# A convolution layer on one core: the order in which bursts of matmuls are written down in layer 1

## The chip, the cores and the metric

The kernel runs on 1 core of one Trainium2 chip. The metric is the device time of one execution, in microseconds (us); the time before is the median of three runs. One more execution was recorded by the hardware profiler: its instructions with their times are the trace, and a page made from it is the profile. The engines are named as there: PE is TensorE (PEld its weight loads), DVE VectorE, ACT ScalarE, POOL GpSimd, SP SyncE, which here only issues DMAs.

## The reference, cut to what matters

Two layers work on `x` of 16 images, 16 channels, 256 x 256 pixels. Layer 0 is a spectral layer (Fourier transforms and residues) and isn't touched. Layer 1 is this, with `B, C, H, W = 16, 16, 256, 256` and `H2 = 128`:

```python
xs = x.reshape(B * C, 1, H, W)                       # x: the group norm of layer 0's output
f = mish(conv2d(xs, W1, b1))                         # 1 -> 4 features, 3x3
top, bot = (f[:, :, :H2], f[:, :, H2:])
ker = conv2d(jax.nn.relu(conv2d(bot, Wred, bred)), Wspan, bspan)     # 4 -> 1 -> 9, 1x1
patches = jax.lax.conv_general_dilated_patches(top, (3, 3), (1, 1), [(1, 1), (1, 1)], ...)
patches = patches.reshape(B * C, 4, K2, H2, W)
top_inv = (patches * ker[:, None]).sum(axis=2)       # the involution
...
shuffled = jnp.concatenate([ti, jnp.roll(bo, -1, axis=1)], axis=3)
shuffled = shuffled.reshape(B, 4 * C, H, W)
out = mish(conv2d(shuffled, W2, b2))                 # 64 -> 16 channels, 3x3
pooled = out.mean(axis=(2, 3))
gate = jax.nn.sigmoid(...)                           # three taps of pooled over the channels
return x * gate[:, :, None, None]
```

The output is `x` plus this. All of it is in 32-bit floats.

## The kernel before

Layer 1 works image by image (`b`), each in nine units (`s` = 0 to 8). One pass of the loop at L1404 is called a step here. A step does one unit of three things at once: the first convolution of the next unit (`nxt`), the involution of this unit (`now`), and one eighth of the second convolution of the image before (`conv2(b - 1, s, acc)`, not in step 8). The first image's steps have no second convolution, the last image's second convolution runs alone at the end in another form (`conv2_last`). Step 8 also begins the gate of the image before (`gated`), whose remaining parts run over the next steps, and makes the first planes of this image (`fresh`).

What TensorE does in a step comes in bursts, each with one shape of array tile:

- `convolve(turn)`, L1130, twice: 24 matmuls with 18 rows and 64 columns of the array, into four PSUM banks (`c1`, in the trace `c`). ScalarE applies mish to the four banks: two into `bot` (L1153), two into `wide` (L1161).
- `involution(kernel)`, L1185, twice: 48 matmuls of 32 x 32 into four banks (`pd`). VectorE multiplies them by `r` into `t` (kernel 0, L1209) or adds `t` to them into `top` (kernel 1, L1211). Kernel 1 then issues `store_top`, eight DMAs on POOL's queue.
- four products, L1268, in `conv2`: 8 matmuls each of 128 x 32 into one bank (`c2ps`). The three taps of a row are computed for pairs of pixels from four planes: differences and sums of neighbouring columns, made by `plane` on VectorE (L1263, two instructions each), with four sets of weights. Product 1 is copied by ScalarE into `a` (L1296), `even` and `odd` gather the four products on VectorE (L1303, L1304, L1307, L1311), and `pooled` (L1286) applies mish to them on ScalarE and sums them up. `following(k)` makes plane `k` for the next step, and may overwrite it once product `k` has read it.
- `reduce`, L1165: 8 matmuls of 64 x 32 into two banks (`pr`), the sum over the rows of `bot`. ScalarE makes `r` of them (L1182), and `store_bot` issues its DMAs on POOL's queue.

A matmul of 32-bit floats is two instructions in the trace, so a product has 16 there, a turn 48, an involution kernel 96.

All these outputs come from one pool of eight PSUM banks, tag `bank` (L1040), in rotation: the ninth request waits until the first bank has been read out. A step with products asks for 4 x 4 + 4 + 2 = 22.

Inside `tc.manual_schedule` (L1397) the order on PE, ACT, DVE and POOL is the order in which the Python code writes instructions down; each engine works its own queue in that order, and semaphores join them where data do. In the kernel before, `conv2` is a generator: at each `yield` it hands back to the loop, which writes something else in between. In this way each product stands between two bursts of other work. `pooled(odd, 1)` is written in the next step, by `next(first, None)`. SP's queue holds `load_rows` (`z`, eight DMAs a unit, three buffers, issued two units ahead by `begin_unit`), `conv2_rows` (one DMA for the rows of a later step, two buffers, so it waits for the planes that read the old ones) and the gate's loads `o`.

Of the kernel before, what the change touches and what calls it, by code (L numbers as in the profile page):

```python
# [10 lines left out]
F32 = mybir.dt.float32  # L11
# [10 lines left out]
P = 128  # L22
# [1001 lines left out]
def layer1(ctx, tc, d, zn, cf, mr, nb):  # L1024
# [8 lines left out]
    H = N // 2  # L1033
# [3 lines left out]
    rp = ctx.enter_context(tc.tile_pool(name="l1r", bufs=3))  # L1037
    op = ctx.enter_context(tc.tile_pool(name="l1o", bufs=4))
    sm = ctx.enter_context(tc.tile_pool(name="l1s", bufs=2))
    banks = ctx.enter_context(tc.tile_pool(name="banks", bufs=8, space=PSUM))  # L1040

    def bank(shape, name):
        return banks.tile([P, *shape], F32, tag="bank", name=name)
# [203 lines left out]
    def conv2_rows(b, s):  # L1247
        t = rows2[(8 * b + s) % 2]
        flat = cf[b % 4].rearrange("(t y) f c x -> (y f c) t x", y=2)
        nc.sync.dma_start(out=t[:, :, 1 : N + 1], in_=flat[:, 16 * s : 16 * s + 17])  # L1250

    def plane(b, s, k):

        t = rows2[(8 * b + s) % 2]
        before, odd, even, after = (t[:, :, x : x + H] for x in (0, 1, H + 1, H + 2))
        x, y, op_ = (
            (before, odd, ALU.subtract),
            (odd, even, ALU.add),
            (odd, even, ALU.subtract),
            (even, after, ALU.subtract),  # L1260
        )[k]
        for rows in (slice(0, 9), slice(9, 17)):
            nc.vector.tensor_tensor(planes[:, k, rows], x[:, rows], y[:, rows], op_)  # L1263

    def conv2(b, s, acc):

        def products(terms):
            ps = bank([4, H], "c2ps")  # L1268
            for i, (w, src) in enumerate(terms):
                for blk in range(2):  # L1270
                    for j in range(4):
                        nc.tensor.matmul(  # L1272
                            ps[32 * j : 32 * j + 32],
                            lhsT=w[:, blk],
                            rhs=src[:, 4 * j + blk : 4 * j + blk + 4],
                            start=(i, blk) == (0, 0),
                            stop=(i, blk) == (len(terms) - 1, 1),
                        )
            return ps

        def product(k):
            return products([(weights[k], planes[:, k])])

        def pooled(y, q):
            k = 2 * s + q
            nc.scalar.activation(y, y, AF.Mish, bias=b2, accum_out=acc[:, k : k + 1])  # L1286

        def following(k):
            if s < 7:
                plane(b, s + 1, k)  # L1290

        if b == nb - 1:
            yield from conv2_last(b, s, products, pooled)
            return
        a = rp.tile([P, 4, H], F32, tag="mid", name="mid", bufs=2)
        nc.scalar.copy(a, product(1))  # L1296
        following(1)
        yield
        ps = product(2)
        even = rp.tile([P, 4, H], F32, tag="even", name="even", bufs=2)  # L1300
        odd = rp.tile([P, 4, H], F32, tag="odd", name="odd", bufs=2)
        yield
        nc.vector.tensor_tensor(even, ps, a, ALU.add)  # L1303
        nc.vector.tensor_tensor(odd, a, ps, ALU.subtract)  # L1304
        following(2)
        yield
        nc.vector.tensor_tensor(even, product(0), even, ALU.add)  # L1307
        following(0)
        yield
        pooled(even, 0)  # L1310
        nc.vector.tensor_tensor(odd, odd, product(3), ALU.subtract)  # L1311
        following(3)
        yield
        pooled(odd, 1)
        yield

    def conv2_last(b, s, products, pooled):

        t = rows2[(8 * b + s) % 2]
        nc.vector.tensor_tensor(pair, t[:, :, H + 1 :], t[:, :, : H + 1], ALU.add)  # L1320
        nc.scalar.copy(mid[:, :, :H], products([(c2[:, :, 1], t[:, :, H + 1 : N + 1])]))
        ps = products([(c2[:, :, 0], t[:, :, :H]), (c2[:, :, 2], t[:, :, 1 : H + 1])])
        even = rp.tile([P, 4, H], F32, tag="even", name="even", bufs=2)
        nc.vector.tensor_tensor(even, ps, mid[:, :, :H], ALU.add)
        odd = rp.tile([P, 4, H], F32, tag="odd", name="odd", bufs=2)
        nc.vector.tensor_tensor(odd, ps, mid[:, :, 1:], ALU.add)
        pooled(even, 0)
        ps = products([(c2[:, :, 0], pair[:, :, :H]), (w12, pair[:, :, 1:])])
        nc.vector.tensor_tensor(odd, ps, odd, ALU.subtract)
        pooled(odd, 1)  # L1330
        yield

    def gate(b, acc):

# [55 lines left out]
    def begin_unit(i):  # L1390
        if i < len(order):
            b, n = order[i]
            units[i] = Unit(b, i, n)

    E = mybir.EngineType
    with tc.manual_schedule(engines={E.PE, E.Activation, E.DVE, E.Pool}):
        begin_unit(0)  # L1397
        begin_unit(1)
        u = units[0]
        u.convolve(0)  # L1400
        u.convolve(1)
        u.reduce()
        acc, last, first, second = None, iter(()), iter(()), iter(())
        for i in range(9 * nb + 12):  # L1404
            b, s = divmod(i, 9)
            now, nxt = units.pop(i, None), units.get(i + 1)
            begin_unit(i + 2)
            if s >= 7 and b < nb:
                conv2_rows(b, s - 7)
            if b == nb and 0 < s < 7:  # L1410
                conv2_rows(b - 1, s + 1)
            if s < 6 and 0 < b < nb:
                conv2_rows(b - 1, s + 2)
            fresh = s == 8 and b < nb - 1
            gated = s == 8 and 0 < b <= nb
            next(last, None)
            if nxt:
                nxt.convolve(0)
            if s < 8 and b and b <= nb:
                if s == 0:  # L1420
                    acc = sm.tile([P, 16], F32, tag="acc", name="acc")
                second = conv2(b - 1, s, acc)
            if now:
                now.involution(0)
            next(first, None)
            next(second, None)
            if now:
                now.involution(1)
            if fresh:
                plane(b, 0, 1)  # L1430
            next(second, None)
            if gated:
                last = gate(b - 1, acc)
                next(last)
            if nxt:
                nxt.convolve(1)
            next(second, None)
            if fresh:
                plane(b, 0, 2)
            next(second, None)  # L1440
            if fresh:
                plane(b, 0, 0)
            if nxt:
                nxt.reduce()
            next(second, None)
            if gated:
                next(last)
            if fresh:
                plane(b, 0, 3)
            if gated:  # L1450
                next(last)
            next(last, None)
            first, second = second, iter(())

# [143 lines left out]
@with_exitstack  # L1600
def forward(ctx, tc, d):
    nb = d["x"].shape[0]
    dram = ctx.enter_context(tc.tile_pool(name="dram", bufs=1, space=DRAM))
    keep = ctx.enter_context(tc.tile_pool(name="keep", bufs=1))
    al = dram.tile([17, 4, 2, C, nb, 2, N], F32, name="al")
    bd = dram.tile([nb, P, P], F32, name="bd")
    hd = dram.tile([2, 2, 64, 2, nb // 2, C, N], F32, name="hd")
    tabs = (
        dram.tile([P, C // 2, 4, N], F32, name="td"),
        dram.tile([NF, P, 384], F32, name="avd"),  # L1610
        dram.tile([P, 2, C, N], F32, name="ed"),
    )
    zn = dram.tile([nb, N + 2, C, N + 2], F32, name="zn")
    cf = dram.tile([4, N + 2, 4, C, N], F32, name="cf")
    mr = keep.tile([P, nb, G, 2], F32, name="mr")
    layer0_forward(tc, d, al, bd, tabs)
    layer0_mix(tc, d, al, hd, tabs)
    layer0_back(tc, d, hd, bd, zn, mr, tabs[2])
    layer1(tc, d, zn, cf, mr, nb)
# [25 lines left out]
```

## Time and profile before

| what | us |
|---|---|
| time before, median of 3 runs (5986.34 to 6002.63) | 5996.09 |
| profiled execution, its own time | 6010.53 |
| its span, first to last instruction | 6008.8 |
| layer 1 in it, 2930.0 to 6008.8 | 3078.8 |
| of which PE busy / DVE busy | 2984.7 / 2282.5 |
| of which ACT busy / POOL busy | 1137.6 / 1512.4 |
| 14 images in their steady course, 3264.7 to 5878.6 | 2613.9 |
| the last image's end, 5878.6 to 6008.8 | 130.2 |

The 16 DMA engines are busy 83% of layer 1 on average, and the mean granted clock of TensorE over the span is 0.978 of full speed. Busy shares are means over stages with different limits; one line of the timeline is a run of equal instructions, with its start, its length and, in brackets, the time that its engine stood idle before it and what ended that. The length of a run of matmuls includes the modelled end of the last one, so the next run can begin before it is over; durations of bursts are therefore taken from start to start.

### The profile page before, as it was taken

What the parts mean: (1) busy time and instruction counts of PE and PEld (TensorE: products, weight loads), DVE (VectorE), ACT (ScalarE), POOL (GpSimd) and SP (SyncE); (2) the same over time, 40 slices, a digit from 0 to 9 for tenths busy, and PEclk for the clock granted to TensorE, in tenths of its full rate; (3) what the DMA queues carried; (4) which work ended last, traced back from release to release, by engine and by line L of the source; (5) the groups of instructions that cost most, each with busy time, mean ns of one, the idle gap of its engine ahead of it and who ended that gap; (6) DMA issues with size and microseconds to landing.
All of it is one profiled execution on the core that took longest, in us unless ns stands there. A gap on an engine that the chain in (4) does not pass through costs nothing.

```text
span 6008.8 us, 216283 instructions
## 1 busy us (share of the span) xinstructions
PE 5572.9 (93%) x94280; PEld 3166.7 (53%) x94280; DVE 4666.5 (78%) x8643; ACT 2310.8 (38%) x4158; POOL 2802.4 (47%) x4090
## 2 busy tenths in 40 slices
PE   6999999688988888999899999999999999999996
PEld 5888888576766766777433333333333333333332
DVE  8888888388887876888557787777877778777784
ACT  2344556344444442222233333333333333333331
POOL 1344444333333335666544555544555445544453
PEclk9999999899999999999899999999999999999998
DMA  3455555566565658999677888888888888888886
GB/s 96 142 141 160 164 143 144 159 189 199 193 200 190 194 193 294 326 327 326 216 217 217 280 269 268 251 242 272 271 267 251 243 268 279 264 250 251 262 278 225
DMA packets 814469, 1370.07 MB, mean 228 GB/s; under 512 B 139824, under 2 KB 629168, under 8 KB 798384
## 3 DMA queue, kind: packets, MB, share of 16 engines
q1 hardware_dynamic: 596176, 881.61, 46.5%
q0 software_dynamic: 217344, 474.61, 25.8%
q8 instruction: 741, 12.14, 0.8%
q14 instruction: 208, 1.70, 0.1%
HBM read 729.78 MB, written 556.47 MB: 214 GB/s over the span
## 4 chain that ended last, share of the span: by engine, by line
PE 66%; DVE 20%; DMA 8%; issue 4%; ACT 1%; POOL 1%; SPq 1%; DVEq 0%; ACTq 0%; POOLq 0%
PE pd L1194 16%; PE c2ps L1272 15%; PE c L1144 12%; DMA z<-in_x 5%; PE ph L760 4%; PE ps L706 3%; PE pg L725 3%; PE pr L1172 2%; DVE planes L1263 2%; PE py L951 2%; PE py L952 2%; DVE st L167 2%; PE pt L741 2%; DVE zb L983 1%; DVE st L968 1%
## 5 line engine op out<-in xcount | busy, mean ns | idle before, releaser
L1224 POOL DMA_DIRECT2D cf<-top x1152 | 668.3, 692 | 1162.8 <-DVE top L1211 987.0
L1263 DVE TENSOR_TENSOR planes<-rows 128x1152 f32<-128x1152 f32 x960 | 1203.4, 1295 | 0.1
L1194 PE MATMUL pd<-wide,dw 32*32 32x512 f32 x27648 | 1032.8, 599 | 32.8 <-issue 17.6
L1153 ACT ACTIVATE bot<-c,b 128x512 f32<-128x512 f32 x576 | 364.8, 684 | 1450.9 <-PE c L1144 1099.4
L1144 PE MATMUL c<-z,w 18*64 18x512 f32 x13824 | 835.1, 601 | 15.7 <-DMA z<-zn 15.7
L1194 PEld LDWEIGHTS pd<-wide,dw 32*32 32x32 f32 x27648 | 446.6, 103 | 595.7 <-issue 455.5
L1209 DVE TENSOR_TENSOR t<-pd,r 128x512 f32<-128x512 f32 x576 | 357.5, 682 | 482.3 <-PE pd L1194 481.7
L1144 PEld LDWEIGHTS c<-z,w 18*64 18x64 f32 x13824 | 293.2, 132 | 533.4 <-issue 410.8
L1242 POOL DMA_DIRECT2D cf<-bot x720 | 395.4, 622 | 198.3 <-DMA cf<-top 81.2
L780 POOL TENSOR_TENSOR h<-w 128x256 f32<-128x256 f32 x258 | 211.4, 820 | 583.7 <-DVE w L774 580.8
L1272 PE MATMUL c2ps<-planes,c 128*32 128x512 f32 x3968 | 477.1, 598 | 0.0
L1211 DVE TENSOR_TENSOR top<-pd,t 128x512 f32<-128x512 f32 x576 | 357.4, 682 | 106.4 <-PE pd L1194 106.1
L1369 POOL TENSOR_SCALAR o<-o,scale,mean 128x258 f32<-128x258 f32 x488 | 355.5, 736 | 155.9 <-DVE scale L1361 141.5
L964 POOL TENSOR_TENSOR x<-x,o 128x512 f32<-128x512 f32 x256 | 324.5, 1268 | 215.1 <-DVE o L963 215.1
L205 PE MATMUL pu<-fy,f 128*128 128x128 f32 x2048 | 414.8, 285 | 1.1 <-ACT u L219 1.0
L212 PE MATMUL pv<-at,f 128*128 128x128 f32 x2048 | 403.1, 279 | 0.0
L322 POOL DMA_DIRECT2D al<-o x544 | 338.3, 629 | 118.1 <-ACT o L313 79.2
L1161 ACT ACTIVATE wide<-c,b 128x512 f32<-128x512 f32 x576 | 365.0, 693 | 0.0
L725 PE MATMUL pg<-alb,s 128*32 128x64 f32 x16896 | 288.0, 222 | 70.7 <-issue 52.3
L706 PE MATMUL ps<-tt,lt 64*32 64x256 f32 x8448 | 292.3, 388 | 54.0 <-issue 20.5
L951 PE MATMUL py<-h,iy 128*128 128x256 f32 x1024 | 316.4, 391 | 10.7 <-DMA h<-hd 10.7
L760 PE MATMUL ph<-ix,yt 64*128 64x128 f32 x4128 | 294.2, 281 | 31.2 <-DVE w L774 22.0
(244 smaller groups left out, 9937.8 us busy)
## 6 DMA issues: line engine op xcount, KB each, us to landing
rows<-cf SPq DMA_DIRECT2D x128, 2176.0 KB
cf<-top POOLq DMA_DIRECT2D x896, 112.0 KB, 5.5
cf<-bot POOLq DMA_DIRECT2D x336, 224.0 KB, 6.4
z<-zn SPq DMA_DIRECT2D x576, 129.0 KB
alb<-alx SPq DMA_DIRECT2D x132, 512.0 KB
zn<-zb SPq DMA_DIRECT2D x128, 516.0 KB
o<-zn SPq DMA_DIRECT2D x128, 516.0 KB
z<-in_x SPq DMA_DIRECT2D x64, 1024.0 KB
```

The source lines that it names most:

```text
L205: nc.tensor.matmul(pu[:, h, :, :, e].rearrange("p v g m -> p (v g) m"), lhsT=f[:, e, c, h], rhs=fy[:, e].rearrange("p (n m) -> p n m", m=2 ...
L212: nc.tensor.matmul(pv[:, a, h], lhsT=f[:, e, c, h], rhs=at[:, e, 4 * cg + c].rearrange("p l m -> p (l m)"), start=e == 0, stop=e == 1,)
L706: nc.tensor.matmul(ps[32 * g : 32 * g + 32, odd, v], lhsT=lt[lanes, kk, g, 1 - v : 3 - v].rearrange("p l c -> p (l c)"), rhs=tt[lanes, kk, g],
L725: nc.tensor.matmul(ps[32 * q : 32 * q + 32, x], lhsT=s[:, i].rearrange("p v k -> p (v k)"), rhs=alb[:, :, column(i)], start=True, stop=True,)
L760: nc.tensor.matmul(ph[q][:, e, blocks], lhsT=yt[lanes, i].rearrange("p t k -> p (t k)"), rhs=ix[lanes, i].rearrange("p (b x) -> p b x", b= ...
L951: nc.tensor.matmul(py[:, e], lhsT=iy[:, e], rhs=h[:, e, k % 4], start=True, stop=False)
L1144: nc.tensor.matmul(ps[half, a][to : to + 64], lhsT=w1[lanes, dx], rhs=self.z[lanes, c : c + 2, dx : dx + N], start=dx == 0, stop=dx == 2,)
L1194: nc.tensor.matmul(out[32 * k : 32 * k + 32], lhsT=dw[lanes, kernel, dx], rhs=self.feat[lanes, 2 * k : 2 * k + 2, dx : dx + N], start=dx == 0,
L1224: nc.gpsimd.dma_start(out=rows[y + 2 * lo : y + 2 * hi, :, c + 2 * k : c + 2 * k + 2].rearrange("y f c x -> y f (c x)"), in_=o[32 * k + 2 ...
L1242: nc.gpsimd.dma_start(out=rows[y + 4 * lo : y + 4 * hi, to : to + n].rearrange("p c x -> p (c x)"), in_=src.rearrange("p c q x -> p (c q x)"),
L1263: nc.vector.tensor_tensor(planes[:, k, rows], x[:, rows], y[:, rows], op_)
L1272: nc.tensor.matmul(ps[32 * j : 32 * j + 32], lhsT=w[:, blk], rhs=src[:, 4 * j + blk : 4 * j + blk + 4], start=(i, blk) == (0, 0), stop=(i, ...
```

## The change

`conv2` loses its `yield`s and is a plain function that writes its four products one after the other, with the sums of `even` and `odd` and both `pooled` between them; the planes 2, 0 and 3 for the next step are written after both. The loop writes the convolution's two turns, then the involution's two kernels, then (in step 8) the gate's second part and the four planes of this image, then `conv2`, then `reduce`. The gate's first part moves to the head of step 8, ahead of the turns, and its matmul `pg` ahead of `reduce`. `pooled(odd, 1)` is no longer put off to the next step. No instruction is added or taken away.

```diff
-            yield from conv2_last(b, s, products, pooled)
+            conv2_last(b, s, products, pooled)
             return
         a = rp.tile([P, 4, H], F32, tag="mid", name="mid", bufs=2)
+        even = rp.tile([P, 4, H], F32, tag="even", name="even", bufs=2)
+        odd = rp.tile([P, 4, H], F32, tag="odd", name="odd", bufs=2)
         nc.scalar.copy(a, product(1))
         following(1)
-        yield
         ps = product(2)
-        even = rp.tile([P, 4, H], F32, tag="even", name="even", bufs=2)
-        odd = rp.tile([P, 4, H], F32, tag="odd", name="odd", bufs=2)
-        yield
         nc.vector.tensor_tensor(even, ps, a, ALU.add)
         nc.vector.tensor_tensor(odd, a, ps, ALU.subtract)
-        following(2)
-        yield
         nc.vector.tensor_tensor(even, product(0), even, ALU.add)
-        following(0)
-        yield
         pooled(even, 0)
         nc.vector.tensor_tensor(odd, odd, product(3), ALU.subtract)
-        following(3)
-        yield
         pooled(odd, 1)
-        yield
+        for k in (2, 0, 3):
+            following(k)
...
-        acc, last, first, second = None, iter(()), iter(()), iter(())
+        acc, last = None, iter(())
...
-            fresh = s == 8 and b < nb - 1
             gated = s == 8 and 0 < b <= nb
             next(last, None)
-            if nxt:
-                nxt.convolve(0)
-            if s < 8 and b and b <= nb:
-                if s == 0:
-                    acc = sm.tile([P, 16], F32, tag="acc", name="acc")
-                second = conv2(b - 1, s, acc)
-            if now:
-                now.involution(0)
-            next(first, None)
-            next(second, None)
-            if now:
-                now.involution(1)
-            if fresh:
-                plane(b, 0, 1)
-            next(second, None)
             if gated:
                 last = gate(b - 1, acc)
                 next(last)
             if nxt:
+                nxt.convolve(0)
                 nxt.convolve(1)
-            next(second, None)
-            if fresh:
-                plane(b, 0, 2)
-            next(second, None)
-            if fresh:
-                plane(b, 0, 0)
+            if now:
+                now.involution(0)
+                now.involution(1)
+            if gated:
+                next(last)
+            if s == 8 and b < nb - 1:
+                for k in (1, 2, 0, 3):
+                    plane(b, 0, k)
+            if s < 8 and b and b <= nb:
+                if s == 0:
+                    acc = sm.tile([P, 16], F32, tag="acc", name="acc")
+                conv2(b - 1, s, acc)
             if nxt:
                 nxt.reduce()
-            next(second, None)
-            if gated:
-                next(last)
-            if fresh:
-                plane(b, 0, 3)
             if gated:
                 next(last)
             next(last, None)
-            first, second = second, iter(())
```

More of the change, by code (lines that the diff above doesn't have):

```diff
@@ L1330, in conv2_last @@
         pooled(odd, 1)
-        yield
     def gate(b, acc):
```

## The prediction

> **What bounds it now.** I read the page first: engine shares, then the chain that ended last.
>
> ```profile
> PE 5572.9 (93%) x94280; PEld 3166.7 (53%) x94280; DVE 4666.5 (78%) x8643; ACT 2310.8 (38%) x4158; POOL 2802.4 (47%) x4090
> PE 66%; DVE 20%; DMA 8%; issue 4%; ACT 1%; POOL 1%; SPq 1%; DVEq 0%; ACTq 0%; POOLq 0%
> ```
>
> TensorE carries the chain, but both lines cover two layers, and only layer 1 (2930 to 6009 us) is edited. So I read the timeline of TensorE over one ordinary step (columns: start, length, engine, line, operation, count).
>
> ```profile
> 4512.06 2.83 PE L1144 MATMUL c<-z,w 18*64 18x512 f32 x48
> 4514.82 3.40 PE L1194 MATMUL pd<-wide,dw 32*32 32x512 f32 x96
> 4518.16 1.92 PE L1272 MATMUL c2ps<-planes,w_sum 128*32 128x512 f32 x16
> 4520.01 3.40 PE L1194 MATMUL pd<-wide,dw 32*32 32x512 f32 x96
> 4523.35 1.92 PE L1272 MATMUL c2ps<-planes,w_difference 128*32 128x512 f32 x16
> 4525.20 2.83 PE L1144 MATMUL c<-z,w 18*64 18x512 f32 x48
> 4527.96 1.92 PE L1272 MATMUL c2ps<-planes,c 128*32 128x512 f32 x16
> 4529.81 1.09 PE L1172 MATMUL pr<-bot,wr 64*32 64x512 f32 x16
> 4530.83 1.92 PE L1272 MATMUL c2ps<-planes,c 128*32 128x512 f32 x16
> 4532.69 0.69 PE L1144 MATMUL c<-z,w 18*64 18x512 f32 x8
> ```
>
> No line has an idle time: each burst starts as the last one ends, and the step is 4532.69 - 4512.06 = 20.63 us. From start to start, a convolution turn (C) takes 2.76, an involution kernel (I) 3.33, a product (P) 1.85, the sum over rows (R) 1.02. Over the same 20.6 us VectorE is busy 17.05 and ScalarE 8.1. So only shorter TensorE work can shorten such a step, and the number of matmuls doesn't change. What is left is the seam between bursts.
>
> **Price of a seam.** Where the old kernel already has equal bursts together, a seam can be read: two involution kernels in a step without products, three products in the last image.
>
> ```profile
> 3267.47 6.60 PE L1194 MATMUL pd<-wide,dw 32*32 32x512 f32 x192
> 3274.00 2.83 PE L1144 MATMUL c<-z,w 18*64 18x512 f32 x48
> ...
> 5898.87 5.43 PE L1272 MATMUL c2ps<-rows,c 128*32 128x512 f32 x48
> 5904.07 1.95 PE L1272 MATMUL c2ps<-planes,c 128*32 128x512 f32 x16
> 5905.78 1.95 PE L1272 MATMUL c2ps<-planes,w 128*32 128x512 f32 x16
> ```
>
> Two I together: 6.53, against 2 x 3.335 = 6.67, so 0.14 for the seam. Products together: 5905.78 - 5904.07 = 1.71 against 1.855, so 0.145. For C-C no warm row exists; within a turn the weight loads follow each other by 0.43, six of these are 2.58 of the 2.76, so its seam is between 0 and 0.18. I take 0.145, what the other two have. The new step is C C, I I, P P P P, R: nine bursts become four, five seams go: 5 x 0.145 = 0.725, and the step becomes 19.90.
>
> **Do the new neighbours wait?** All matmul outputs share 8 PSUM banks in rotation. I put C at 0, then C 2.61, I 5.37, I 8.6, P from 11.9, R 18.9. The ends come from rows of the old step: ScalarE starts on a turn 2.84 after its start (4525.20, 4528.04):
>
> ```profile
> 4528.04 1.27 ACT L1153 ACTIVATE bot<-c,b 128x512 f32<-128x512 f32 x2 [7.28 <-PE c L1144]
> 4529.19 1.27 ACT L1161 ACTIVATE wide<-c,b 128x512 f32<-128x512 f32 x2
> ```
>
> - The first I takes the banks of the first C. Fourth bank free at 2.84 + 1.15 + 1.27 = 5.26, plus 0.06 (old waits resume TensorE that soon): 5.32, needed 5.37. It fits by 0.05. Bounds: 0 to 0.15 lost per step; I take 0.
> - The second I takes the second C's: 5.46 + 2.42 = 7.9, needed 8.6.
> - VectorE: t 8.83 to 11.3 (3.46 after the first I starts, as at 4514.82/4518.28), top 11.9 to 14.4, plane 1 to 16.9, the four sums to 19.8, planes 2, 0, 3 to 27.2, which is 7.3 of the next step; t is due there at 8.8. Slack 1.5. Planes 2, 0, 3 are read from 13.6 on, so they are early.
> - Second C of the next step takes the banks of P0, P3 and R. R's are read last, behind both pooled activations: odd sum 19.8, pooled to 20.7, r to 21.9; needed 22.5.
>
> The Trainium skill (Trainium Kernel Development and Optimization, Best Practices) speaks against the change: tiling speeds TensorE up, not the emptying of PSUM, and two turns together fill all eight banks. By that rule the involution would wait for the whole eviction; by the rows above ScalarE empties the first four while the second turn runs. The rule's sum is my slow rival; the rows' is 0.05 to spare.
>
> **Queues passed.** SP's rows load waits for plane 3 of the step before, so it moves from 2.7 to 7.3 in its step, but its reader (plane 1, one step on) moves from 8.6 to 14.4: the lead stays about 26 us. z loads behind it lead by over a step. POOL keeps its order; store_top comes at 13.6, store_bot after R. The gate's sum moves to the head of the step, which saves 0.2 of TensorE's wait per image.
>
> **Turn of the image** (steps 8, 0, 1). Old: 15.0 (3264.71 to 3279.71), 23.94 (to 3303.65), then 20.6. New step 8: 5.37 + 6.53 + 0.3 (pg) + 1.02 = 13.2, since R no longer stands behind the second turn's activation (2.4 there, 1.02 behind other work). But VectorE is late: top ends 14.4, the gate's 16 small operations to 17.7, eight plane halves (9.9) to 27.6, scale to 28.3, that is 15.1 into step 0. t is due at 8.8 and starts at 15.1; the first product takes t's bank, so it waits from 12.0 to 15.8. That is an added wait of 3.9 us; behind it on TensorE stand all products, R and the next turn. Step 0: 15.8 + 6.98 + 1.02 = 23.8. By that alone step 1 would lose 1.2, because R's banks come late to its second C.
>
> A gap that long also costs clock, as an instruction gap in the first image shows (windows: start:end, length, busy and count of five engines, clock, DMA share, GB/s):
>
> ```profile
> 3025.95 1.47 PE L1194 MATMUL pd<-wide,dw 32*32 32x512 f32 x33 [2.22 <-issue]
> 3027.34 5.08 PE L1144 MATMUL c<-z,w 18*64 18x512 f32 x48
> ...
> 3028.90:3032.40 3.50, 3.50 (x42) 0.82 (x28) 0.81 (x2) 0.01 (x1) 3.50 (x7) 0.50 0.79 198
> ```
>
> After 2.22 us idle the granted clock is 0.50 for some 6 us: C takes 5.08 for 2.83, R 2.82 for 2.44, 2.6 lost. A gap of 1.29 at 3058.8 cost as much, one of 0.91 at 2979.5 nothing. The skill's rule (TensorE: Matmul & The Clock Gate, HAM oscillation) is that gaps above about 3.4 us halve the clock for a window of 3.4, which would cost 1.7. The row decides: 2.6. Step 0 becomes 26.4; then R comes so late that step 1's wait for R's banks is covered, and step 1 is 19.9. Turn: -1.8 + 2.5 - 0.7 = 0. Without the clock drop it would be -1.8 - 0.1 + 0.5 = -1.4.
>
> **First image, 8 steps without products.** Old 14.43 (2989.34 to 3003.77). New 5.37 + 6.53 + 1.02 + 0.25 (the first C waits for the second I's bank) = 13.15. Saved 1.28 each. **Last image**: bursts unchanged, rows wait for DMA there; 0 (at most 3, where pg waited for the sum).
>
> **Sum.** Steps 2 to 7 of 15 images: 90 x 0.725 = 65. Turns: 15 x 0 = 0. First image: 8 x 1.28 = 10. Together 75 of the profiled span: 6008.8 to 5934, execution 6010.5 to 5935.5. The median shown is 14 below that execution; the same 75 off 5996 gives **5921**, 1.25% less.
>
> **Rivals.**
> - *DMA caps the steps behind the gate.* For: after a turn the DMA engines are full:
>
> ```profile
> 3303.65:3324.50 20.85, 20.64 (x372) 7.10 (x368) 16.93 (x21) 7.62 (x16) 14.01 (x23) 1.00 1.02 333
> ```
>
>   Against: outside the last image no plane ever waited for rows. If three steps an image can't shorten: 15 x 3 x 0.725 = 33 back, 5954. Chance 0.12.
> - *The turn eats the gain.* The gap in step 0 longer, or VectorE's lag still there in steps 2 and 3: 5 us per image give all of it back, 5996. Against: VectorE regains 2.3 us per step. 0.08.
> - *ScalarE doesn't free the first turn's banks before the second turn ends* (slower). Then the fourth bank comes at 5.46 + 2.42 = 7.9, I waits 2.5, in every one of 143 steps: 358 lost less 75, 6279, and more if the clock falls. It decides from 0.7 us of lateness per step. Against: the old ScalarE starts within 0.1 of a turn's end with the next burst already running. 0.12.
> - *Seams cost the same whatever stands beside* contradicts the rows above; it lies in the second rival's result.
>
> **Chances.** Forecast 0.68, the rivals 0.12, 0.08, 0.12. Forecast's bounds: no clock drop 21 lower, C-C seam at 0.18 another 4; 0.15 at the first I, 20 higher. With the DMA case on top of that: 5892 to 5976. Faster by over 0.3% (about what can be told from no change): 0.68 + 0.12 = 0.80; same 0.08; slower 0.12.
>
> **What would show it.** In an ordinary step: period 19.9, 96 c, 192 pd, 64 c2ps matmuls in unbroken runs, no idle at the first pd. In step 0: c2ps idle about 3.9 behind t, clock 0.5 after it. In the first image 13.2. Wrong if pd waits for ACT wide by more than 0.7, or planes wait for rows.

## The result

| | us |
|---|---|
| kernel before, median of 4 runs (5973.89 to 6002.63) | 5991.22 |
| changed kernel, median of 4 runs (5903.02 to 5926.36) | 5913.39 |
| ratio, 95% interval | 0.9874 (0.9841 to 0.9906) |
| profiled execution of the changed kernel, and its span | 5909.9, 5908.1 |

The forecast was 75 us less; the medians differ by 78. The page of the changed kernel, the same two lines as before:

```profile
PE 5447.1 (92%) x94280; PEld 3319.2 (56%) x94280; DVE 4671.7 (79%) x8643; ACT 2324.0 (39%) x4158; POOL 2831.1 (48%) x4090
PE 55%; DVE 10%; issue 2%; DMA 1%; ACT 1%; POOL 0%; SPq 0%; DVEq 0%; ACTq 0%; POOLq 0%
```

The instruction counts are the same, to the last one. TensorE is busy 126 us less, which is not faster matmuls: the tail of a run's last matmul covers the seam behind it, so a seam counts as busy time, and there are fewer seams. The span is 100.7 us shorter, so TensorE is also idle for 25 us more. An ordinary step in the changed kernel's timeline of TensorE:

```profile
3102.90 5.41 PE L1144 MATMUL c<-z,w 18*64 18x512 f32 x96
3108.24 6.60 PE L1194 MATMUL pd<-wide,dw 32*32 32x512 f32 x192
3114.77 1.92 PE L1272 MATMUL c2ps<-planes,w_sum 128*32 128x512 f32 x16
3116.51 1.90 PE L1272 MATMUL c2ps<-planes,w_difference 128*32 128x512 f32 x16
3118.22 3.62 PE L1272 MATMUL c2ps<-planes,c 128*32 128x512 f32 x32
3121.77 1.09 PE L1172 MATMUL pr<-bot,wr 64*32 64x512 f32 x16
3122.79 5.41 PE L1144 MATMUL c<-z,w 18*64 18x512 f32 x96
```

3122.79 - 3102.90 = 19.89 us, and no line has an idle time. Start to start: two turns 5.34 (2 x 2.76 = 5.52 before), two involution kernels 6.53 (6.67), four products 7.00 (7.42), the sum 1.02. The five seams are worth 0.18 + 0.14 + 0.42 = 0.74.

A usual turn of an image, from the head of step 8 to the head of step 1:

```profile
5232.97 5.41 PE L1144 MATMUL c<-z,w 18*64 18x512 f32 x96
5238.31 6.60 PE L1194 MATMUL pd<-wide,dw 32*32 32x512 f32 x192
5244.84 0.39 PE L1345 MATMUL pg<-wca,totals 128*128 128x16 f32 x2
5245.16 1.09 PE L1172 MATMUL pr<-bot,wr 64*32 64x512 f32 x16
5246.18 6.00 PE L1144 MATMUL c<-z,w 18*64 18x512 f32 x96
5252.11 6.60 PE L1194 MATMUL pd<-wide,dw 32*32 32x512 f32 x192
5261.63 3.62 PE L1272 MATMUL c2ps<-planes,w_sum 128*32 128x512 f32 x16 [2.92 <-DVE t L1209]
5265.03 1.94 PE L1272 MATMUL c2ps<-planes,w_difference 128*32 128x512 f32 x16
...
5271.35 5.41 PE L1144 MATMUL c<-z,w 18*64 18x512 f32 x96
```

Step 8 takes 13.21. In step 0, 25.17 long, the first product waits 2.92 us for VectorE's `t`, and then takes 3.40 instead of 1.7. The clock behind that wait, in the windows view (the third last number):

```profile
5261.58:5265.18 3.60, 3.55 (x20) 0.99 (x24) 3.60 (x7) 0.00 (x0) 3.26 (x7) 0.53 0.98 332
```

Where the 100.7 us between the two spans came from:

| stretch | before | after | difference |
|---|---|---|---|
| up to layer 1's first step (the code is the same) | 2955.7 | 2940.7 | -15.0 |
| first image, steps 0 to 7 | 127.6 | 108.9 | -18.8 |
| its step 8, and the second image to its step 8 | 181.4 | 172.7 | -8.8 |
| 14 images from step 8 to step 8 | 2613.9 | 2559.5 | -54.4 |
| end of the last image | 130.2 | 126.4 | -3.8 |

The first row isn't the change's: it varies from one execution to the next, and a later kernel with the old order (E2) had 2934.6 there. That leaves 86 us in layer 1. The first image gained 18.8, and not the 10 forecast, because the old execution had three steps there of 16.3, 19.7 and 19.3 us with instruction gaps like the one that the prediction showed; of the new steps one has such a gap (16.1), the others take 12.9 to 13.6.

By step, the mean over 13 images (head of one step to the next; the last of the 14 isn't complete):

| step | 8 | 0 | 1 | 2 | 3 | 4 | 5 | 6 | 7 | sum |
|---|---|---|---|---|---|---|---|---|---|---|
| before | 15.07 | 23.99 | 21.30 | 20.92 | 21.47 | 21.27 | 21.23 | 20.71 | 20.84 | 186.80 |
| after | 13.47 | 24.71 | 21.40 | 21.13 | 20.95 | 20.63 | 20.32 | 19.91 | 20.15 | 182.67 |

Seams alone would give 0.74 in each of the steps 1 to 7. Steps 6 and 7 have it; steps 1 to 4 have little of it.

### The profile page after: what moved, and what is told of

Its sections match the earlier page's. It is cut to its first block, busy times and chain, and to the rows that moved or that the text cites. A ratio compares the mean times of both kernels' runs of the same rounds, so it can differ in the third digit from the quotient of the medians.

```text
span 5908.1 us, 216564 instructions
## 1 busy us (share of the span) xinstructions
PE 5447.1 (92%) x94280; PEld 3319.2 (56%) x94280; DVE 4671.7 (79%) x8643; ACT 2324.0 (39%) x4158; POOL 2831.1 (48%) x4090
## 4 chain that ended last, share of the span: by engine, by line
PE 55%; DVE 10%; issue 2%; DMA 1%; ACT 1%; POOL 0%; SPq 0%; DVEq 0%; ACTq 0%; POOLq 0%
PE c2ps L1272 15%; PE pd L1194 15%; PE c L1144 12%; DVE planes L1263 2%; PE pr L1172 2%; PE py L951 2%; PE py L952 2%; PE ph L760 2%; PE ps L706 2%; DVE zb L983 1%; DVE st L968 1%; PE pg L725 1%; PE pf L940 1%; PE pt L741 1%; DVE o L963 1%
## 5 line engine op out<-in xcount | busy, mean ns | idle before, releaser
L1263 DVE TENSOR_TENSOR planes<-rows 128x1152 f32<-128x1152 f32 x960 | 1180.4, 1293 | 7.0 <-PE c2ps L1272 6.9
L1194 PE MATMUL pd<-wide,dw 32*32 32x512 f32 x27648 | 988.6, 597 | 28.2 <-issue 28.0
L1144 PE MATMUL c<-z,w 18*64 18x512 f32 x13824 | 801.5, 595 | 16.2 <-DMA z<-zn 15.8
L1194 PEld LDWEIGHTS pd<-wide,dw 32*32 32x32 f32 x27648 | 542.2, 103 | 459.4 <-issue 175.2
L1144 PEld LDWEIGHTS c<-z,w 18*64 18x64 f32 x13824 | 319.6, 131 | 491.0 <-issue 352.0
L1361 POOL TENSOR_SCALAR o<-o,scale,mean 128x258 f32<-128x258 f32 x488 | 386.1, 799 | 151.6 <-DVE scale L1353 133.6
L1272 PE MATMUL c2ps<-planes,c 128*32 128x512 f32 x3968 | 454.7, 594 | 3.4 <-DVE planes L1313 3.4
L1298 ACT COPY mid<-c2ps 128x512 f32<-128x512 f32 x120 | 70.5, 588 | 867.3 <-PE c2ps L1272 867.3
```

Source lines behind the costliest of these rows:

```text
L1144: nc.tensor.matmul(ps[half, a][to : to + 64], lhsT=w1[lanes, dx], rhs=self.z[lanes, c : c + 2, dx : dx + N], start=dx == 0, stop=dx == 2,)
L1194: nc.tensor.matmul(out[32 * k : 32 * k + 32], lhsT=dw[lanes, kernel, dx], rhs=self.feat[lanes, 2 * k : 2 * k + 2, dx : dx + N], start=dx == 0,
L1272: nc.tensor.matmul(ps[32 * j : 32 * j + 32], lhsT=w[:, blk], rhs=src[:, 4 * j + blk : 4 * j + blk + 4], start=(i, blk) == (0, 0), stop=(i, ...
L1361: eng.tensor_scalar(o[:, i], o[:, i], scale[:, c + i : c + i + 1], mean2[:, b, c + i : c + i + 1], ALU.mult, ALU.add,)
```

## The experiments

The theory is the prediction's: the gain is the seams, five in an ordinary step; the turn is held up by VectorE's lag and the clock. The rivals: the gain comes from waits that went, not from seams; the turn is bound by something else; the steps behind the gate are bound by the DMA engines. In each run the period of an ordinary step is that of the undisturbed steps, the commonest length, which repeats to 0.01 us.

**E4, E8: seams put back one by one.** In `conv2` of the changed kernel:

```diff
         following(1)
+        yield                      # E4: C C I P I P P P R
         ps = product(2)
...
+        between()                  # E8: nxt.reduce(), C C I I P P R P P
         nc.vector.tensor_tensor(even, product(0), even, ALU.add)
```

> The changed kernel with product 1 put back between the two involution kernels: C C I P I P P P R, six bursts for four. Seams: one of I-I and one of P-P more, 0.14 each: an ordinary step takes 20.17 for 19.89. Rival (the step shortened because waits went, not because of the seams): no wait comes back here, so 19.89.

> The changed kernel with the sum over rows put between products 2 and 0: C C I I P P R P P, five bursts for four. One seam more: an ordinary step takes 20.03 for 19.89. Rival (waits, not seams): 19.89, since R's input and its banks are ready there.

Measured: 20.17 and 20.03, both to the hundredth. With the changed kernel's 19.89 at four bursts and the old 20.63 at nine, the step follows the number of bursts, 0.14 to 0.15 for each. Neither run brought a wait back in these steps. Times of one execution each: 5946.9 and 5915.0.

**E5, E6: is it the shape?** Ahead of products 2, 0 and 3 one more small matmul, once of the products' shape, once of another:

```diff
+            if k != 1:
+                extra = bank([4, H], "extra")
+                nc.tensor.matmul(extra[:32, 0], lhsT=weights[0][:, 0], rhs=planes[:, k, 0], start=True, stop=True)
```

E6 has `[:32, 0]` and `[:32, k, 0]` for the two operands.

> The changed kernel with one added matmul of 128 columns ahead of products 2, 0 and 3, of the products' own tile shape (128 rows, 32 columns of the array), into a bank that nobody reads. This is the control of the next run: the added matmuls cost their own length, at most 3 x 0.21 us, so an ordinary step takes 20.0 to 20.6.

> As the control, but the three added matmuls use 32 rows of the array instead of 128. If the seam is the price of another tile shape, each of them opens one or two seams of 0.14 that the control doesn't have: an ordinary step is 0.4 to 0.85 us longer than the control's. If the seam belongs to the boundary between two operations whatever their shapes, the two runs agree within 0.05.

Measured: 20.53 with the same shape (0.213 for each added matmul, its own length), 21.30 with the other: 0.77 more, or 0.26 for each pair of seams (one execution each, 5962.0 and 6050.2). So it is the change of shape, and not the boundary between two operations. The weight loads show how. In the timeline of TensorE's weight loads (here of E1) the first load of a burst of another shape comes 0.84 after the last, one of the same shape 0.30:

```profile
3795.43 0.16 PEld L1272 LDWEIGHTS c2ps<-planes,w_sum 128*32 128x32 f32 x8 [0.84 <-DVE t L1209]
...
3796.75 0.13 PEld L1272 LDWEIGHTS c2ps<-planes,w_difference 128*32 128x32 f32 x4 [0.30 <-DVE top L1211]
```

The first line is the seam from involution to product, the second the boundary between product 1 and 2; both first loads have a releaser named, and only one costs. The 0.30 is also the distance within one product. The loads of product 2 thus begin 0.43 ahead of its first matmul in the ordinary step above (3116.08 and 3116.51); those of product 1, behind the seam, begin with it (3114.76 and 3114.77).

**E7: how much room has ScalarE?** One more copy between the two pairs of mish of the first turn:

```diff
+            if turn == 0:
+                spare = rp.tile([P, 4, H], F32, tag="spare", name="spare", bufs=1)
+                nc.scalar.copy(spare, self.bot[:, 0:2].rearrange("p c e x -> p (c e) x"))
             for a in range(2):
```

> The changed kernel with one more copy on ScalarE (about 0.59 us) between the two pairs of mish of the first turn. Theory: the involution needs the first turn's fourth bank only 0.05 us after it is free, so an ordinary step becomes 0.5 us longer, 20.4. Rival (the banks have room): 19.89.

Its ordinary step in the timeline of TensorE:

```profile
4525.84 5.41 PE L1144 MATMUL c<-z,w 18*64 18x512 f32 x96
4531.17 7.05 PE L1197 MATMUL pd<-wide,dw 32*32 32x512 f32 x192
```

The involution starts as soon, but its run is 0.45 longer, since its fourth bank comes late: 20.34 (20.4 forecast, 19.89 by the rival). In all undisturbed steps of the changed kernel that bank is free 5.31 us into the step, and the first matmul into it runs at 5.36; with the copy it is free at 5.78, and the matmul runs at 5.79. The room was 0.05, as forecast. One execution took 5945.8.

**E1, E3: VectorE's lag in the turn.** The planes of the next image are made in step 7, all four (E1) or plane 1 alone (E3):

```diff
-            if s == 8 and b < nb - 1:
-                for k in (1, 2, 0, 3):
-                    plane(b, 0, k)
...
                 conv2(b - 1, s, acc)
+            if s == 7 and b < nb - 1:
+                for k in (1, 2, 0, 3):
+                    plane(b, 0, k)
```

> The changed kernel, with the four planes of the next image made at the end of step 7, where VectorE has none to make, instead of in step 8. Theory (the turn is held up by VectorE's lag, and then by the clock): step 8 stays 13.2 us, step 0 falls from 25.0 to 19.9, no idle of TensorE behind t, clock 1.0, step 1 19.9 plus its instruction gaps. That is 5 to 6 us for each of 14 images: about 5835 us, some 0.974 of the kernel before. Rival (the turn is bound by the DMA engines, which are full after it): step 0 stays above 23 and the time within 20 us of 5913. Ordinary steps 19.89 by both.

> The changed kernel with only plane 1 of the next image made in step 7, planes 2, 0 and 3 still in step 8. Theory with the clock: VectorE's lag is 2.5 us less, TensorE's idle time in step 0 falls from about 3.2 to about 0.6, too short to cost clock, and step 0 falls from 25.0 to about 21 (2.6 of idle time and 1.4 of slow clock). Rival without a cost of clock: step 0 falls by the idle time alone, to 22.4.

E3 did what was expected (5877.9 in one run). The first product of a step 0 in the timeline of TensorE:

```profile
5232.31 1.92 PE L1272 MATMUL c2ps<-planes,w_sum 128*32 128x512 f32 x16 [0.45 <-DVE t L1209]
```

And the whole of that step in the windows view:

```profile
5219.33:5240.34 21.01, 20.56 (x377) 9.23 (x369) 20.36 (x40) 6.69 (x11) 15.72 (x24) 1.00 0.74 219
```

2.5 us less of VectorE's work ahead of `t` leave 0.45 of the wait, the clock stays at 1.00, and step 0 has a median of 21.03 for 25.04: 4.0 less for 2.5 moved, where a wait without a price in clock would have left 22.4.

E1 moved the other three as well and should have gone to 19.9. It measured 5864.9 (5 runs), 0.9783 of the kernel before (0.9761 to 0.9805): better than both kernels, by less than forecast. No wait for `t` is left, but step 0 has a median of 22.65. What came in its place, in the timeline of TensorE:

```profile
3961.82 5.41 PE L1144 MATMUL c<-z,w 18*64 18x512 f32 x96
3967.15 1.07 PE L1194 MATMUL pd<-wide,dw 32*32 32x512 f32 x11
3969.80 6.50 PE L1194 MATMUL pd<-wide,dw 32*32 32x512 f32 x181 [1.57 <-issue]
3976.23 1.92 PE L1272 MATMUL c2ps<-planes,w_sum 128*32 128x512 f32 x16
```

The two involution kernels take 9.08 for 6.53, with a stop after 11 of 192 matmuls that waits for nothing the profile shows ("issue"). The time thus went into gaps of TensorE's own, the kind that the next experiments are about. Neither forecast of E1 came out: step 0 was to be 19.9, or above 23 by the rival.

**E2: the same move in the old order.**

> The kernel before with the same move of the four planes into step 7, bursts still apart. Theory: ordinary steps stay at 20.63, step 8 at 15.05, step 0 falls from 23.95 to about 20.7: 3.3 us for each of 14 images, about 5945 us, 0.992 of the kernel before. Beside the run with the bursts together it leaves 0.74 for a step with products, 1.85 for step 8 and 1.2 for a step of the first image, together about 110 us. Rival (part of the gain of the change came from where VectorE's work stands, not from the seams): ordinary steps fall below 20.5.

Ordinary steps stayed at 20.63, so the place of VectorE's work has no part in the gain of the change. The rest was wrong: 6050.2, or 1.0092 of the kernel before (1.0072 to 1.0112), step 8 took 20.3 for 15.05, and step 0, which was to fall to 20.7, has a median of 24.4. The timeline of its step 8, TensorE and VectorE:

```profile
3619.83 9.70 DVE L1263 TENSOR_TENSOR planes<-rows 128x1152 f32<-128x1152 f32 x8
3621.85 6.60 PE L1194 MATMUL pd<-wide,dw 32*32 32x512 f32 x192
...
3629.45 2.48 DVE L1209 TENSOR_TENSOR t<-pd,r 128x512 f32<-128x512 f32 x4
3630.19 7.17 PE L1144 MATMUL c<-z,w 18*64 18x512 f32 x48 [1.74 <-DVE t L1209]
```

In the old order the involution follows the first turn at once, so `t` is due 6.2 us into step 8, not 8.8; eight plane halves in front of it make it 4.1 late, the second turn waits for its bank, and the clock falls (0.50 from 3633 to 3639): 7.17 for a turn of 2.83. The same move gains in one order and loses in the other.

**E9, E10, E11: where do the gaps come from?** In the changed kernel "issue" holds TensorE up in the involution bursts for 28.0 us of layer 1, in E1 for 44.5. The theory was the DMA engines, full in steps 1 to 4. One part of the gate per step instead of two, in E1 (E9), the changed kernel (E10) and the kernel before (E11):

```diff
             gated = s == 8 and 0 < b <= nb
-            next(last, None)
```

> The kernel of the first experiment (planes of the next image in step 7), with one part of the gate per step for six steps instead of two per step for three, so that its loads and stores (8 MB per image) lie wider apart. Theory (in the steps behind the gate the DMA engines are full, and TensorE's instructions then come late, in the dense involution bursts): the DMA share of steps 1 to 4 falls from 1.00 to about 0.9, the time that the involution bursts take over 6.53 us falls from some 88 us in 14 images to less than half, about 5820 us. Rival (the gaps belong to places in the instruction stream, whatever the DMA engines do): they stay at 80 or more and the time within 10 us of 5865.

> The changed kernel with the gate spread in the same way, planes left in step 8. Theory: steps 1 to 4 fall from a mean of 21.0 towards 20.2, about 5880 us; step 0 keeps its wait behind VectorE. Rival: within 10 us of 5913.

> The kernel before with the gate spread in the same way. Theory: its involution bursts, over 80 us longer than their 3.34 each in 14 images, lose half of that: about 5960 us. Beside the changed kernel with the gate spread this gives the price of the five seams where the DMA engines are less full: 80 to 90 us. Rival: within 10 us of the kernel before.

By the times the theory failed: 5879.8, 5913.0 and 5995.4, ratios to the kernel before 0.9799 (0.9781 to 0.9816), 0.9864 (0.9845 to 0.9883) and 0.9995 (0.9983 to 1.0007). E10 and E11 lie where the rival put them; E9 is 15 us above E1, outside both forecasts. The traces say more, as five steps of E10 show (steps 1 to 5 of one image; the second last number is the DMA share):

```profile
3804.15:3825.45 21.30, 20.50 (x377) 8.00 (x369) 17.18 (x21) 8.25 (x16) 11.26 (x21) 1.00 1.03 334
3825.45:3845.34 19.89, 19.89 (x377) 8.01 (x369) 17.27 (x21) 8.15 (x16) 16.31 (x22) 1.00 0.79 271
3845.34:3867.37 22.03, 20.71 (x376) 7.42 (x369) 17.16 (x21) 8.22 (x16) 7.08 (x13) 1.00 0.97 295
3867.37:3887.26 19.89, 19.89 (x376) 8.02 (x369) 17.07 (x21) 8.23 (x16) 15.97 (x24) 1.00 0.78 258
3887.26:3908.94 21.68, 20.87 (x376) 7.81 (x368) 17.06 (x21) 8.22 (x16) 7.05 (x13) 1.00 0.97 295
```

The edit didn't lower the share evenly: every second step is full now, for longer, up to step 7. And the gaps went along: full steps are 1.4 to 2.1 us too long, the others 19.89 exactly. So the premise of the expectation (0.9 everywhere) wasn't met, and the gaps aren't tied to fixed steps. GpSimd, whose work on the gate the edit moves too, is busy for 16 us in the steps without gaps and for 7 in two of the full ones, so its work isn't what stops TensorE here.

**E12: less to move.** E1 with `for k in range(0, 8 if b == nb - 1 else 2, 2)` in `gate`, and no loads of further parts. It leaves out three quarters of the output of 15 images, with GpSimd's work on them.

> The kernel of the first experiment, which for 15 of the 16 images scales and stores only the first quarter of the channels (the other three quarters of the output are left out), so that 6.2 MB of loads and stores per image go. TensorE's, VectorE's and ScalarE's work for layer 1 is the same. Theory (TensorE's gaps come from full DMA engines): steps 1 to 7 have a DMA share below 0.9 and take 19.89 each, the involution bursts' excess over 6.53 us in 14 images falls from 88 us to below 30, about 5790 us. Rival (the gaps belong to places in the instruction stream): the excess stays above 60 and the time above 5840.

5816.2 in one run, between the two forecasts; so is the involution bursts' excess over 6.53 us each, 39 us (E1: 89). Steps 1 to 7 have a median of 19.89 or 19.90 each. Of what is left, 25 us are in step 0, still 22.4. Sorting the steps 1 to 7 (97 steps of 14 images) by their DMA share, with their mean length over 19.89 (20.63 for the kernel before and E11):

| kernel | share below 0.9: steps, us over | share from 0.95: steps, us over | sum over all, us |
|---|---|---|---|
| before | 41, 0.30 | 50, 0.61 | 45 |
| changed | 37, 0.10 | 49, 1.31 | 75 |
| E1 | 35, 0.06 | 50, 1.14 | 68 |
| E12 | 74, 0.15 | 12, 0.55 | 18 |
| E9 | 32, 0.06 | 54, 0.85 | 50 |
| E10 | 37, 0.13 | 53, 1.04 | 67 |
| E11 | 26, 0.41 | 28, 0.45 | 41 |

In the new order the gaps come with full DMA engines. In the old order they do so less, and in E11 not at all. A full step costs the changed kernel 0.7 more than the old one: of the 0.74 that its seams give, nearly all.

**What TensorE lacks in the gaps.** The traces of the runs answer this. The page of the changed kernel lists two DMA queues of the kind "instruction"; the larger one (packets, MB, share of the 16 engines):

```profile
q8 instruction: 740, 12.12, 0.9%
```

These are 740 packets of 16 KB. TensorE's instructions, weight loads and semaphore instructions counted, are 189628, which is 256 for each packet: this queue brings TensorE its instructions. Counted from one packet to the next, each of the 33 stops for "issue" in the changed kernel from 2960 us on comes exactly where 256 instructions have been used up, and ends 1.2 to 1.6 us after the next packet has landed. In the 14 traces together it is 387 stops of 387, at the same place of the count, ending 1.2 to 1.9 us after a packet (a moment taken at random is 1.1 to 1.9 us behind one in 11% of cases). The stop of E1 shown above ends at 3969.80; its packet landed at 3968.02. Delays that the timeline doesn't show as idle go the same way: each of the 50 steps 1 to 7 of the changed kernel (the kernel before: 40) that are over 0.1 us too long has a packet that TensorE began to use within 1.95 us of its landing; of the 45 that are on time 19 have one. So what is late is TensorE's instructions.

The change makes this worse by itself. As an estimate from the rows above and the prediction's, two involution kernels in one run use 256 instructions in 4.4 us (384 in 6.53); in the old order, an involution kernel, a product and the head of the next kernel take 5.7. No run tests that estimate alone, and why a packet is late at one place and not at another stays open.

## Why the prediction was right

**Seams.** 0.725 for five forecast, 0.74 measured; two were read from the old trace to 0.005, the one without a row (two turns, taken at 0.145) is 0.18, the upper bound that the prediction gave. E4, E5, E6 and E8 show that number and shape make it.

**ScalarE and PSUM.** Forecast to fit by 0.05 (bank free at 5.32, needed at 5.37); measured 5.31 and 5.36. The rule of the Trainium skill (Trainium Kernel Development and Optimization, Best Practices), that tiling doesn't speed the emptying of PSUM up, is true here as a limit one would meet next, as in E7, and not as a cost of this change.

**The turn.** Step 8 13.2 forecast, 13.21 measured. `t` started 14.6 us into step 0 (median; 15.1 forecast), and the first product at 15.4 (15.8). The clock's price was mis-sized: 2.6 was taken from a row in which the clock was down for some 6 us. In 3 of the 14 turns the clock stayed at 1.00, and step 0 took 22.1 to 23.4; in ten it was down for about 3.4 us, the four products took 8.4 to 8.7 instead of 7.0, and the step 24.9 to 25.3; in one, with the clock down for longer, 9.9 and 26.7. The usual price is thus 1.4 to 1.7. The Trainium skill (TensorE: Matmul & The Clock Gate, Part 1 and HAM oscillation) has half speed for a window of about 3.4 us, from which the prediction's 1.7 is an estimate, and that was the better figure. Its rule that only idle times above about 3.4 us matter was not: 1.29 us in the old trace and 1.74 in E2 were enough. Step 0 was therefore lower than forecast (24.7 on average for 26.4), and the turn gained 0.8 where 0 was forecast.

**Steps 1 to 4.** This is the term that was too high: 0.725 was taken for all steps 2 to 7, 4.35 an image; they gave 3.35, and step 1 nothing instead of 0.7. The first rival had named the place and given it 33 us. By the table above it took some 30, so it happened beside the forecast case and not in its stead. Its argument against ("no plane waited for rows") looked at the wrong victim: not the planes' data but TensorE's instructions came late.

**The sum** is in part luck, because the misses cancel: a whole image gained 3.9 for 4.35 (54 us of 61 over 14 images), since steps 2 to 7 fell short by 1.0 and the turn made up for most of it; and the first image gained 9 us more than forecast, for gaps that the old execution happened to have. The outer bounds, 5892 and 5976, are a little off their own terms, which add up to 5896 and 5974.

**Rivals.** ScalarE freed the banks in time; the turn did not eat the gain; the seams are real.

## What to carry to other kernels

Where TensorE is the bound and its timeline has no idle times, count the changes of tile shape: each cost 0.13 to 0.18 us here, and they can be priced beforehand wherever the old trace has equal bursts side by side. Before moving work together, walk each buffer's release and each queue through one step and through the irregular step: the ordinary step came out to 0.01 us by hand, and both surprises sat where the load is uneven. Joining dense bursts also raises the rate at which an engine uses up its instructions, so look at the queue that brings them. When a wait is removed, ask which other resource is full in that very stretch: E1 took a 3 us wait away and got back less than it had cost, and E2 shows the same move losing in another order.

## What the runs showed of the hardware

- In these traces weight loads run ahead into the next burst if it has the same tile shape and not if it has another: 0.30 us from the last load against 0.81 to 0.84 at a seam, and three matmuls of another shape cost 0.77 us more than three of the same (E5, E6).
- An idle time of TensorE of 2.1 to 3.3 us behind `t` cost 1.4 to 1.7 us of clock on top in ten turns, 2.9 in one, none in three; 0.45 us cost none (E3). Length alone doesn't decide: a stop of 1.29 us took the clock to 0.50 in the kernel before, and stops of up to 2.67 us left it at 1.00 in E1.
- TensorE's instructions arrive in packets of 256, and each of the 387 stops for "issue" from 2960 us on in the 14 traces falls on the end of one. They last 0.2 to 3.2 us and are commonest in dense involution bursts (192 matmuls in 6.53 us).
- In the new order these stops come mostly with DMA engines that are 95% busy or more over the step (1.31 us a step, 0.10 below 90%); moving the DMA load to other steps moved them (E10), taking it away took most of them (E12). The mean over a step can hide a full stretch: in step 0 of E1, E9 and E12 it is 0.8 to 0.9, but 0.94 on average in the 5 us before a stop.
